# Four heads at a time in two cross attentions, a new order in the latents' attention, and half of X's norm first, in a Perceiver kernel of twelve blocks

## The chip, the cores and the metric

The kernel runs on one core of a Trainium2 chip, in one launch. The metric is device time in microseconds (us); less is better. A core has a matrix engine, TensorE (PE in profiles, with its weight loads under PEld), a vector engine (DVE), a scalar engine (ACT), GpSimd (POOL) and SyncE (SP), which here only issues DMAs. PE writes to PSUM; the other engines copy from there to SBUF, the working memory. Each engine has its own instruction stream and waits on semaphores for the others.

## The reference

Sixteen batch elements of 64 latent tokens with 256 channels (`x`) attend to 1024 context tokens of 192 channels, in four rounds of attention to the context, a mixing layer and a feed-forward layer:

```python
x = x + _L0_xattn_ref(_layernorm(x), ctx, ...)      # 16 heads of 16
x = x + _L0_attn_ref(_layernorm(x), ...)            # then _L0_ffn_ref
x = x + _L1_xattn_ref(_layernorm(x), ctx, ...)      # 8 heads of 64
x = x + _L1_attn_ref(_layernorm(x), ...)            # then _L1_ffn_ref
x = x + _L2_xattn_ref(_layernorm(x), ctx, ...)      # 8 heads of 64
x = x + _L2_attn_ref(_layernorm(x), ...)            # then _L2_ffn_ref
x = x + _L3_xattn_ref(ctx, _layernorm(x), mask, ...)  # 4 heads of 64
x = x + _L3_attn_ref(_layernorm(x), ...)            # then _L3_ffn_ref
```

The first three cross attentions are softmax attentions with the products

```python
q = (x @ Wq).reshape(B, Sq, h, d).transpose(0, 2, 1, 3)
k = (context @ Wk).reshape(B, -1, h, d).transpose(0, 2, 1, 3)
v = (context @ Wv).reshape(B, -1, h, d).transpose(0, 2, 1, 3)
attn = softmax(einsum('bhid,bhjd->bhij', q, k) * scale)
out = einsum('bhij,bhjd->bhid', attn, v)            # then @ Wo
```

The fourth normalises the context, takes keys and values from both context and latents (1024 + 64 keys), divides queries and keys of each head by their root mean square, and masks part of the context.

## The kernel before

All is float32. `X` holds the 1024 tokens as eight tiles of 128 x 256. The blocks run one after the other (`BLOCKS`); the change touches three of their functions, and `network`, which loads X.

**What orders the work.** A framework sorts the instructions into each engine's stream by a simulated time, and a piece of text that stands earlier goes first among what is ready. Where a block has called `set_order(True)`, every matrix instruction through `mm` (L188) and `tr` (L191, a transpose by the identity), and every DVE and ACT instruction through `dve` and `act` (all recorded at L72), keeps the order of the text on its engine. Instructions through `nc.vector`, `nc.gpsimd` and the DMA issues are outside that order. Tiles come from pools with a given number of buffers; a new tile waits until the last user of its buffer is done.

**First attention, `xattn_direct` (L281 on).** Weights wq, wk, wv, wo are loaded through POOL's queue; two value tiles of 128 x 4096 are zeroed on POOL (L313), since each head's 16 value channels stand in a block of 32. `norm_T` normalises all of X: `layernorm` takes statistics of tiles (L220, L221), roots on POOL (`rsqrt`, L205 and L206, for tiles 0 to 3, 4 to 6 and 7), normalises (L227), and transposes each half (L251) into `xnT`. Then `queries(0, c)` for the first eight batch elements, the four pieces of `project(0, piece)` (two of keys, two of values), and 64 steps over (element, four heads): scores (two PSUM tiles), negated maxima (`least`, nm), exponentials (`exps`, with their sums), division (`shares`), transposes, and the values of the step before. Steps 4 to 7 take the queries of the other eight elements.

**Cross attentions two and three, `xattn_folded` (L479 on).** The key weights are folded into the queries (`qw`), so scores are taken with the context itself: `cT` is its transpose, with 128 channels as full rows and the other 64 stored in two row halves for two halves of the keys; `cx` is the context as it is. There are 64 steps (b, r), r being a pair of heads. `scores` fills one PSUM tile of 128 x 1024: two products over 128 rows, then two over 64 rows, which run side by side in the two row halves of the array (64*128 in the profile). `transposes` turns the probabilities into `pT`, through two PSUM buffers (`ps_t`), the first half copied by ACT, the second by DVE. `values(b - 1, r)` multiplies two key tiles of the element before: full products into `o0`, and products of 64 columns into `o1`, of which two run side by side (128*64). A step is

```python
nxt = scores(*ahead)
transposes(pTs[b][:, :, r * P : (r + 1) * P], pr)
nxt = exps(*nxt)
values(b - 1, r)
pr = shares(*nxt)
```

`ps_s` has two buffers for scores; so have `cT`, `cx` and `pT`. Attention three also calls `ctx_sigma` for each element at its load, which takes the context's statistics with `nc.vector` (L277, L278: eight of each), outside the order. Attention two works on the taps of the next block's convolution in steps 6 to 23 (`conv_taps`, POOL, ACT, POOL, DVE in turn) and issues `tap_rows` DMAs later. Every eighth element new queries are folded (`fresh`).

**Latents' attention, `xattn3` (L1448 on).** One pass over 16 elements. In the pass of element b the four pieces of keys and values of b + 1 are projected (`project`, pkv; DVE evicts), squared on ACT, summed on DVE and rooted on POOL (`roots`, L1522 and L1523), scaled on DVE (`scale`), and transposed (`keys_T`); the latents' own keys take the same way (`latents`, `lat`). `last_T` turns the last keys of b + 1 and the last probabilities of b, `probs_T` the other probabilities, `values` multiplies. `mid` has seven PSUM buffers.

Of the kernel before, what the change touches and what calls it, by code (L numbers as in the profile page):

```python
# [78 lines left out]
class Net:  # L79
# [201 lines left out]
    def xattn_direct(self, L):  # L281
# [10 lines left out]
        H = 16  # L292
        wq = self.w(a[f"{L}_Wq"].rearrange("(k p) n -> p k n", p=P), [P, 2, D], "wq")
        wk = self.w(a[f"{L}_Wk"].rearrange("(k p) n -> p k n", p=P), [P, 2, D], "wk")
        wv = self.w(a[f"{L}_Wv"].rearrange("(k p) n -> p k n", p=P), [P, 2, D], "wv")
        wo = self.w(a[f"{L}_Wo"].rearrange("(k p) n -> p k n", p=P), [P, 4, D], "wo")
        with ExitStack() as es:
# [12 lines left out]
            vs = []  # L310
            for i in range(2):
                v = one.tile([P, NKC, H, 32], F32, name=f"v{i}")
                nc.gpsimd.memset(v, 0.0)  # L313
                vs.append(v)

            self.norm_T(ps_t, "t")
# [19 lines left out]
            for c in range(4):  # L336
                queries(0, c)
# [99 lines left out]

            self.set_order(True)
            for piece in range(4):
                project(0, piece)  # L440
            steps = [(b, c) for b in range(B) for c in range(4)]
            pss = scores(0, 0)
            prs = [exps(pss[e], least(pss[e])) for e in range(2)]
            for p in prs:
                shares(*p)
            last = None
            for i, (b, c) in enumerate(steps):
# [18 lines left out]
                transposes(pT[:, :, 1, :], prs[1][0], 1, act.copy)  # L466
                if 4 <= i < 8:
                    queries(1, i - 4)
# [10 lines left out]
    def xattn_folded(self, L):  # L479
# [14 lines left out]
        with ExitStack() as es:  # L494
# [52 lines left out]
            def scores(b, r):  # L547
                if r == 0:
                    load(b)
                c0, c1 = ctxs[b]  # L550
                qw = qws[b // G]
                ps = ps_s.tile([P, S], F32, tag="s", name="pss")
                ql = [qw[:, i, b % G, 2 * r : 2 * r + 2, :].rearrange("p h q -> p (h q)") for i in range(2)]
                for n in range(2):
                    cols = slice(n * 512, (n + 1) * 512)
                    self.mm(ps[:, cols], ql[0], c0[:, cols], True, False)
                for n in range(2):
                    cols, rows = slice(n * 512, (n + 1) * 512), slice(n * 64, (n + 1) * 64)
                    self.mm(ps[:, cols], ql[1][rows], c1[rows, :], False, True)
                nm = self.small.tile([P, 1], F32, tag="nm", name="nm", bufs=4)  # L560
                dve.tensor_reduce(nm, ps, AX.X, ALU.max, negate=True)
                return ps, nm

            def exps(ps, nm):
                pr = thr.tile([P, S], F32, tag="pr", name="pr")
                sm = self.small.tile([P, 1], F32, tag="sm", name="sm", bufs=4)
                act.activation(pr, ps, AF.Exp, bias=nm, accum_out=sm)
                return pr, sm
# [14 lines left out]
            def values(b, r):  # L583

                if r == 0:
                    outs[b] = [ps_o.tile([P, 512], F32, tag=n, name=n) for n in ("o0", "o1")]
                o0, o1 = outs[b]
                for j in (2 * r, 2 * r + 1):
                    self.mm(o0, cxs[b][:, j, 0:P], pTs[b][:, j, :], j == 0, j == NKC - 1)
                for j in (2 * r, 2 * r + 1):  # L590
                    rows = slice((j % 2) * 64, (j % 2 + 1) * 64)
                    self.mm(o1[rows, :], cxs[b][:, j, P:C], pTs[b][:, j, :], j < 2, j >= NKC - 2)
# [33 lines left out]
            steps = [(b, r) for b in range(B) for r in range(4)]  # L626
            pr = shares(*exps(*scores(0, 0)))
            for i, (b, r) in enumerate(steps):
# [6 lines left out]
                transposes(pTs[b][:, :, r * P : (r + 1) * P], pr)  # L635
                if fresh:
                    nxt = scores(*ahead)
                if ahead:
                    nxt = exps(*nxt)
                if b > 0:  # L640
                    values(b - 1, r)
                    if r == 3:
                        keep(b - 1)
                if ahead:
                    pr = shares(*nxt)
                if b == 1 and r == 0:
                    self.add_row(f"{L}_bo", one)
                if r == 0 and b % G2 == 1 and b > 1:
                    output(b // G2 - 1)
                if L == "L1_xattn":  # L650

                    if i == 6:
                        taps = self.conv_taps(one, dve, act)
                    if 6 <= i < 24:
                        next(taps)
                    if 28 <= i < 28 + TQ // 2:
                        self.tap_rows(2 * (i - 28))
                        self.tap_rows(2 * (i - 28) + 1)
            for r in range(4):
                values(B - 1, r)  # L660
            keep(B - 1)
# [786 lines left out]
    def xattn3(self):  # L1448
# [14 lines left out]
        with ExitStack() as es:  # L1463
# [5 lines left out]
            if not hasattr(self, "wx"):  # L1469
                self.context_weights()(mid)  # L1470
# [122 lines left out]
            def last_T(b, keys, prs):  # L1593

                pt = mid.tile([P, 512], F32, tag="m", name="ptl")
                if keys:
                    for c in range(2):
                        turn(pt, c, pair(b, NKC, c))
                if prs:
                    st["pT"] = one.tile([P, 2, KT, P], F32, tag="pT", name="pT")  # L1600
                    for c in range(2):
                        turn(pt, 2 + c, prs[c][:, S:])
                    act.copy(st["pT"][:, :, NKC, :], pt[:, 2 * P :].rearrange("p (c q) -> p c q", c=2))
                if keys:
                    act.copy(st["kT"][:, :, S:], pt[:, : 2 * P].rearrange("p (c k) -> p c k", c=2))
# [124 lines left out]
            last_T(0, True, None)  # L1730
# [3 lines left out]
            for b in range(B):  # L1734
# [21 lines left out]
                if more:  # L1756
                    p0, lat = roots(*p0), roots(*lat)
                    p1 = project(b + 1, 1)
                    scale(*p0)
                dve.reciprocal(sums, sums)  # L1760
                if more:
                    p1 = square(*p1)
                act.mul(prs[0], prs[0], sums[:, 0:1])
                if more:
                    p1 = roots(*p1)
# [4 lines left out]
                if more:  # L1770
                    p2 = project(b + 1, 2)
                    scale(*p1)
# [3 lines left out]
                    keys_T(b + 1, 0, act.copy)  # L1776
                act.mul(prs[1], prs[1], sums[:, 1:2])
                if 1 <= b <= 3:
                    q = roots(*q)
                if more:  # L1780
                    p2 = roots(*square(*p2))
                    late = project(b + 1, 3)
                last_T(b + 1, more, prs)
                probs_T(0, prs[0])
                if more:
                    late = square(*late)
                    keys_T(b + 1, 1, dve.tensor_copy)
                    late = roots(*late)
                    scale(*p2)
                if 1 <= b <= 3:  # L1790
                    scale(*q)
                probs_T(1, prs[1])
                values(b, 0)
                if more:
                    keys_T(b + 1, 2, dve.tensor_copy)
# [4 lines left out]
                values(b, 1)  # L1800
# [745 lines left out]
def network(ctx: ExitStack, tc: tile.TileContext, a, out, blocks=BLOCKS):  # L2546
    n = Net(ctx, tc, a)
    for t in range(NT):
        tc.nc.sync.dma_start(out=n.X[:, t, :], in_=a["x"][t * P : (t + 1) * P, :])
# [27 lines left out]
```

## Time and profile before

| | us |
|---|---|
| median of 3 runs | 3303.53 |
| lowest, highest | 3290.88, 3317.2 |
| the profiled execution | 3300.39 |
| its span | 3298.7 |
| PE busy in it | 3085.0 (94%) |
| DVE busy | 1857.1 (56%) |
| ACT busy | 1213.9 (37%) |
| POOL busy | 723.5 (22%) |

The profile is of one execution. A group's row gives an engine, an operation, the tile written and the tile read (out<-in), how often, and its duration. In a timeline the columns are the start and the duration in us, the engine, the line and operation, the tiles, and in brackets how long the engine had been idle and what released it; equal instructions in a row are merged (x8). A window's row is the busy time of PE, PEld, DVE, ACT and POOL with the number of instructions in brackets, then the granted TensorE clock (1 is full speed), the DMAs' share and GB/s. A matrix instruction's recorded duration overlaps the next one's, so starts are compared, not durations. The mean granted clock was 0.959.

Where the stages touched lie in the span: first attention from the start to about 514 us, cross attention two from 755 to 1263, three from 1693 to 2201, the latents' attention from 2596 to 3007.

### The profile page before, as it was taken

To read this page: it belongs to the slowest core of one execution; us is meant where nothing else is said; L and a number is where in the kernel's file an instruction comes from. 1 tells how busy PE (TensorE), PEld (TensorE's weight loads), DVE (VectorE), ACT (ScalarE), POOL (GpSimd) and SP (SyncE) were. 2 spreads that over 40 slices of the span, in tenths; PEclk is the share of its full clock that TensorE was granted. 3 is DMA by queue.
4 is the path that set the end of the run, shared out by engine and by line. 5 is a ranking of instruction groups with operands and counts; after the bars stand their busy time and mean duration, and the time that the engine had idled before them with its cause. 6 is when DMAs were issued, how large, how long until landed. Compare 5 with 4: busy or idle time off the path is not lost.

```text
span 3298.7 us, 48631 instructions
## 1 busy us (share of the span) xinstructions
PE 3085.0 (94%) x20064; PEld 1753.1 (53%) x20064; DVE 1857.1 (56%) x3497; ACT 1213.9 (37%) x2093; POOL 723.5 (22%) x786
## 2 busy tenths in 40 slices
PE   7999999999999999979969999998999899998787
PEld 4666665664344344468834434434665454455676
DVE  6888885424444445961135545557884677775521
ACT  3555554213322221003322232228861254544211
POOL 1000003311200001014410000023771354441131
PEclk9999999999999999969989999998998999999889
DMA  2100000012122113027821111101111111110233
GB/s 71 32 29 30 31 24 11 20 48 79 58 76 73 59 38 78 20 84 288 294 89 58 49 52 54 48 17 34 45 52 34 64 61 55 58 51 14 83 110 118
DMA packets 64511, 213.63 MB, mean 65 GB/s; under 512 B 16433, under 2 KB 27556, under 8 KB 57378
## 3 DMA queue, kind: packets, MB, share of 16 engines
q1 hardware_dynamic: 37296, 106.13, 9.6%
q0 software_dynamic: 21840, 99.39, 9.0%
q10 hardware_dynamic: 5154, 5.01, 0.5%
q8 instruction: 159, 2.61, 0.3%
q14 instruction: 62, 0.51, 0.1%
HBM read 201.62 MB, written 12.66 MB: 65 GB/s over the span
## 4 chain that ended last, share of the span: by engine, by line
PE 78%; DVE 8%; issue 5%; POOL 5%; ACT 3%; DMA 1%; POOLq 0%; DVEq 0%; SPq 0%; ACTq 0%
PE pss L188 14%; PE o L188 13%; PE pst L191 8%; PE pu L188 6%; PE psp L188 5%; PE pd L188 5%; PE py L188 4%; PE psc L188 3%; POOL rnk L1523 2%; PE po L188 2%; PE pb L191 2%; PE psq L188 1%; PE pkv L188 1%; DVE pr L72 1%; DVE kk L72 1%
## 5 line engine op out<-in xcount | busy, mean ns | idle before, releaser
L72 DVE TENSOR_REDUCE nm<-pss 128x1 f32<-128x1024 f32 x256 | 307.4, 1222 | 349.6 <-PE pss L188 349.6
L72 ACT COPY pT<-pst 128x512 f32<-128x512 f32 x256 | 149.8, 585 | 688.8 <-PE pst L191 688.5
L188 PE MATMUL pss<-cT,qw 128*128 128x512 f32 (+1 forms) x1024 | 387.8, 628 | 1.6 <-ACT qw L72 1.6
L188 PE MATMUL o<-pT,cx 128*128 128x512 f32 (+1 forms) x1024 | 370.5, 606 | 0.0
L191 PEld LDWEIGHTS pst<-ident,pr 128*128 128x128 f32 x2048 | 219.8, 141 | 159.1 <-issue 100.1
L72 ACT ACTIVATE pr<-pss,nm 128x1024 f32<-128x1024 f32 x256 | 285.1, 1114 | 34.4 <-DVE nm L72 21.0
L191 PE MATMUL pst<-ident,pr 128*128 128x128 f32 x2048 | 281.0, 280 | 5.7 <-DVE v L72 1.6
L188 PEld LDWEIGHTS pss<-cT,qw 128*128 128x128 f32 (+1 forms) x1024 | 125.8, 187 | 251.1 <-issue 239.4
L188 PEld LDWEIGHTS o<-pT,cx 128*128 128x128 f32 (+1 forms) x1024 | 112.6, 162 | 166.3 <-issue 145.0
L72 DVE TENSOR_SCALAR pr<-pr,sm 128x1024 f32<-128x1024 f32 x256 | 193.1, 754 | 9.0
L188 PE MATMUL pkv<-wx,cT 128*128 128x512 f32 (+1 forms) x512 | 190.2, 623 | 0.6 <-issue 0.6
L205 POOL TENSOR_SCALAR rs<-mv 128x8 f32<-128x8 f32 (+3 forms) x53 | 10.2, 193 | 802.3 <-DVE mv L221 400.3
L72 DVE COPY pT<-pst 128x512 f32<-128x512 f32 x256 | 174.5, 682 | 8.6 <-PE pst L191 4.5
L72 DVE TENSOR_TENSOR_SCAN h<-dA,pb 128x512 f32<-128x512 f32 x128 | 154.7, 1217 | 15.9 <-PE pb L191 9.0
L1347 POOL TENSOR_TENSOR h<-h,cb 128x1024 f32<-128x1024 f32 x64 | 151.4, 2367 | 53.3 <-DVE h L72 51.3
L188 PE MATMUL pd<-wd,hT 128*128 128x256 f32 x656 | 149.3, 382 | 3.0 <-DVE hT L2391 1.4
L2203 DVE TENSOR_SCALAR y<-pd,row 128x256 f32<-128x256 f32 x39 | 18.9, 484 | 223.7 <-PE pd L188 223.7
L188 PEld LDWEIGHTS pd<-wd,hT 128*128 128x128 f32 x656 | 123.1, 190 | 31.3 <-DVE hT L2391 6.2
L1523 POOL TENSOR_TENSOR rnk<-rnk,mhalf 128x8 f32<-128x8 f32 (+1 forms) x84 | 130.2, 1550 | 7.0
L188 PE MATMUL py<-h,ident 128*128 128x512 f32 x256 | 131.1, 598 | 0.0
L188 PEld LDWEIGHTS pu<-xT,up 128*128 128x128 f32 x736 | 110.8, 192 | 21.8 <-ACT hT L2197 14.6
L188 PE MATMUL pu<-xT,up 128*128 128x128 f32 x736 | 121.2, 290 | 1.1 <-DVE xT L2189 0.5
(511 smaller groups left out, 5195.6 us busy)
## 6 DMA issues: line engine op xcount, KB each, us to landing
cT<-in_ctxT SPq DMA_DIRECT2D x64, 768.0 KB, 4.4
cx<-in_ctxP SPq DMA_DIRECT2D x32, 768.0 KB, 4.3
offb<-d_off SPq DMA_DIRECT2D x16, 576.0 KB, 3.7
cb<-d_C SPq DMA_DIRECT2D x16, 512.0 KB, 3.6
wu<-in_L_ffn_w POOLq DMA_DIRECT2D x8, 1024.0 KB, 5.7
wd<-in_L_ffn_w POOLq DMA_DIRECT2D x8, 1024.0 KB, 6.3
wc<-in_L_attn_conv_wT POOLq DMA_DIRECT2D x4, 1024.0 KB, 10.2
T<-d_T SPq DMA_DIRECT2D x8, 512.0 KB, 18.5
```

The costliest lines, as they stand in the source:

```text
L72: ins = getattr(self.engine, op)(*args, **kwargs)
L188: self.in_order(self.nc.tensor.matmul(out, lhsT=lhsT, rhs=rhs, start=start, stop=stop))
L191: self.in_order(self.nc.tensor.transpose(out, in_, self.ident))
L205: nc.gpsimd.tensor_scalar(t[:p, :n], in_, scale, eps, ALU.mult, ALU.add)
L1347: nc.gpsimd.tensor_tensor(hs[i], hs[i], cbs[hf, g], ALU.mult)
L1523: nc.gpsimd.tensor_tensor(r, r, self.mhalf[:, : n * H], ALU.pow)
L2203: nc.vector.tensor_scalar(y[:, i, :], po[:, i * D : (i + 1) * D], weight[:, g + i : g + i + 1], None, ALU.mult)
```

## The change

- First attention: wk is loaded before wq; X's tiles 4 to 7 come through ACT's DMA queue instead of SP's; only the half of the value tiles that values don't fill is zeroed, the second tile's after the first root. The norm is split: `norm(0)` and `normed(0)` for tiles 0 to 3 at the front, `norm(1)` in step 1 and `normed(1)` in step 2. The first two pieces of `project` come before the first queries, the other two after the first scores.
- Cross attentions two and three: 32 steps (b, h) of four heads. `scores` fills both PSUM tiles: full products of both, then the 64-row products of both. `values` keeps the full products; the 64-column products of an element are in `others`, once for each element. `pr` gets four buffers. The taps are taken two to a step in steps 3 to 11.
- Latents' attention: reciprocals and products of the two probability tiles are taken one at a time, `scale`, `keys_T`, `probs_T` and `values` stand in another order, `last_T` is split into `latents_T` and `last_T`, and the copies of the second and third keys go from DVE to ACT. The test for `wx` falls away; the weights are prepared in an earlier block either way.

```diff
-        for t in range(NT): tc.nc.sync.dma_start(out=n.X[:, t, :], ...)
+        (tc.nc.sync, tc.nc.scalar)[t // 4].dma_start(out=n.X[:, t, :], ...)
@@ xattn_direct
-                nc.gpsimd.memset(v, 0.0)
-            self.norm_T(ps_t, "t")
-            for c in range(4):
-                queries(0, c)
-            for piece in range(4):
-                project(0, piece)
+            nc.gpsimd.memset(vs[0][:, :, :, 16:], 0.0)
...
+            norm(0)
+            ins = nc.gpsimd.memset(vs[1][:, :, :, 16:], 0.0)
+            tc.add_manual_dep(ins.ins, self.last_root.ins.name, order, reason="after the norm")
+            normed(0)
+            project(0, 0)
+            project(0, 1)
+            for c in range(4):
+                queries(0, c)
             pss = scores(0, 0)
             prs = [exps(pss[e], least(pss[e])) for e in range(2)]
+            project(0, 2)
+            project(0, 3)
...
+                if i == 1:
+                    norm(1)
+                if i == 2:
+                    normed(1)
@@ xattn_folded
+                for ps, q in zip(pss, ql):
+                    for n in range(2):
+                        self.mm(ps[:, cols], q[0], c0[:, cols], True, False)
+                for ps, q in zip(pss, ql):
+                    for n in range(2):
+                        self.mm(ps[:, cols], q[1][rows], c1[rows, :], False, True)
...
+            def others(b):
+                for j in range(NKC):
+                    rows = slice((j % 2) * 64, (j % 2 + 1) * 64)
+                    self.mm(outs[b][1][rows, :], cxs[b][:, j, P:C], pTs[b][:, j, :], j < 2, j >= NKC - 2)
...
+                    nxt = scores(*ahead)
+                transposes(pTs[b][:, :, at[0]], prs[0])
+                if ahead and not fresh:
+                    nxt = [exps(*x) for x in nxt]
+                if b > 0:
+                    values(b - 1, 2 * h)
+                transposes(pTs[b][:, :, at[1]], prs[1])
+                if fresh:
+                    nxt = [exps(*x) for x in scores(*ahead)]
+                if b > 0:
+                    values(b - 1, 2 * h + 1)
+                    if h == 1:
+                        others(b - 1)
+                        keep(b - 1)
+                if ahead:
+                    prs = [shares(*x) for x in nxt]
@@ xattn3, one pass, the new order
+                dve.reciprocal(sums[:, 0:1], sums[:, 0:1])
+                act.mul(prs[0], prs[0], sums[:, 0:1])
+                    p1 = project(b + 1, 1)
+                dve.reciprocal(sums[:, 1:2], sums[:, 1:2])
+                    p1 = square(*p1)
+                act.mul(prs[1], prs[1], sums[:, 1:2])
+                    scale(*p0)
+                    p1 = roots(*p1)
+                    p2 = square(*project(b + 1, 2))
+                    scale(*lat)
+                    p2 = roots(*p2)
+                    late = project(b + 1, 3)
+                probs_T(0, prs[0])
+                    keys_T(b + 1, 0, act.copy)
+                last_T(prs)
+                    late = square(*late)
+                probs_T(1, prs[1])
+                    scale(*p1)
+                    late = roots(*late)
+                    scale(*p2)
+                    latents_T(b + 1)
+                    keys_T(b + 1, 1, act.copy)
+                values(b, 0)
+                values(b, 1)
+                    keys_T(b + 1, 2, act.copy)
+                    scale(*late)
```

## The prediction

> **What bounds the kernel now.** I read the page's busy shares and its chain first, then the windows of each stage, then the timelines inside the touched stages.
>
> ```profile
> PE 78%; DVE 8%; issue 5%; POOL 5%; ACT 3%; DMA 1%; POOLq 0%; DVEq 0%; SPq 0%; ACTq 0%
> ```
>
> TensorE (PE) ends the chain for 78% of the span, so a stage gains only where its PE stream gets shorter or stops waiting. The windows of cross attention two, cross attention three and the latents' attention (length, then PE, PEld, DVE, ACT and POOL busy):
>
> ```profile
> 755.00:1262.60 507.60, 498.23 (x1853) 210.53 (x1854) 221.61 (x362) 148.18 (x258) 40.59 (x57) 0.99 0.21 65
> 1693.00:2200.60 507.60, 497.97 (x1852) 210.10 (x1852) 252.55 (x590) 143.17 (x240) 48.40 (x56) 0.99 0.14 48
> 2596.20:3006.50 410.30, 369.84 (x2752) 193.41 (x2752) 294.34 (x719) 199.23 (x343) 192.93 (x225) 0.98 0.15 53
> ```
>
> The first two are PE from end to end; the third leaves PE idle for 40 us. But "busy" hides something: the weight loads (PEld) of one step of attention two.
>
> ```profile
> 886.18 0.30 PEld L188 LDWEIGHTS pss<-cT,qw 128*128 128x128 f32 x2 [0.81 <-issue]
> 886.71 0.19 PEld L188 LDWEIGHTS pss<-cT,qw 128*128 128x128 f32 x1 [0.24 <-issue]
> ...
> 888.09 0.30 PEld L188 LDWEIGHTS pss<-cT,qw 64*128 64x128 f32 x4 [0.76 <-issue]
> 889.15 0.86 PEld L191 LDWEIGHTS pst<-ident,pr 128*128 128x128 f32 x8 [0.76 <-issue]
> 889.97 0.30 PEld L188 LDWEIGHTS o<-pT,cx 128*128 128x128 f32 x2
> 890.51 0.19 PEld L188 LDWEIGHTS o<-pT,cx 128*128 128x128 f32 x1 [0.24 <-issue]
> ...
> 891.89 0.20 PEld L188 LDWEIGHTS o<-pT,cx 128*64 128x64 f32 x4 [0.76 <-issue]
> 892.90 0.19 PEld L188 LDWEIGHTS pss<-cT,qw 128*128 128x128 f32 x1 [0.81 <-ACT tapp L72]
> ```
>
> Each f32 product is two passes, and full-array passes follow at 0.43 us. At a change of tiling the load is not hidden: four full passes from 886.18 to 888.09 take 1.91, not 1.72; the 64-row pairs 1.06, not 0.86; eight transposes and the first load 0.93, not 0.87; the next full passes (PE from 890.08) 1.81; the 64-column pairs 1.01, not 0.86. That is 0.69 us of 6.72 per step, 0.35 for each excursion into a 64-row or a 64-column tiling.
>
> **The change part by part.**
>
> *Attentions two and three.* Now each of 64 steps makes one row excursion (scores) and one column excursion (values). Then 32 double steps make one row excursion each, and `others` makes one column excursion per batch element: 48 instead of 128. 80 x 0.347 = 27.8 us per attention, all on PE.
>
> Is the new step fed? I lay it out from its start S with the durations above. Score sums end at 4.75 and 5.6; DVE nm 4.8 to 7.2 (two take 2.36); PE transposes 5.55 to 6.48, values to 8.19, second transposes to 9.07, values to 10.8. ACT: pT copy at 6.15, exponentials 6.75 to 9.2, pT copy 9.25. DVE: pT copy 7.2 to 7.85, then 9.25 to 9.9, the two shares to 11.7. The second transposes need the buffer that DVE's copy frees at 7.85; they come at 8.19/8.63: slack 0.8. Both score tiles are free at 9.2, needed at 10.8. The shares are due at 16.3. Hidden, then. Attention two's taps, two per step: their chain POOL 0.62, ACT 0.41, POOL 1.18, DVE 0.42, twice, ends near 14.8 with the next nm ready at 15.3 (20.1 against 19.3 after a longer step, which the 0.8 of slack covers): nothing. Here the skill has a rule against the change: "TensorEngine Tiling (Array Packing)", section PSUM Bottleneck, warns that once tiling speeds up PE the copies out of PSUM can become the bound, which would make this part 0. The row says DVE is busy 221.61 of 507.60; I keep 27.8.
>
> *Costs of doing two at a time.* The first scores and their exponentials now occupy both score buffers, so PE waits 1.8 us for the first to free; in the first batch element, which has no values between its transposes, the second transposes wait 1.25 twice. Against 0.6 now: -3.7 per attention. Attention two: +24.
>
> *Attention three has a guest.* `ctx_sigma` runs on DVE outside the ordered queue:
>
> ```profile
> 1881.89 1.23 DVE L72 TENSOR_REDUCE nm<-pss 128x1 f32<-128x1024 f32 x1 [2.44 <-PE pss L188]
> 1883.25 0.62 DVE L277 BATCH_NORM_STATS2 st<-cx 128x6 f32<-128x192 f32 x2
> ...
> 1885.82 0.66 DVE L72 COPY pT<-pst 128x512 f32<-128x512 f32 x1
> ```
>
> The context's load is issued when the old values end (1878.92, with S at 1878.80) and its 16 small operations (2.65 us) start on landing, 4.4 later, ahead of the pT copy. Today the next transposes come 6.7 us apart and hide this. In the new step they land at S+4.45, before the first nm: nm 7.1 to 9.5, copy to 10.2, and the second transposes, due at 8.63, start at 10.3. That is 1.65 us of PE wait for each of the 14 batch elements whose context waits for a buffer: -23. If the operations fall behind one or both nm it is 2.0 (-28); if behind the pT copy, nothing. I take -23: attention three +1.
>
> A wait can also cost clock. Windows of 3.41 us, the granted clock being the third number from the end:
>
> ```profile
> 2623.66:2627.07 3.41, 1.65 (x11) 1.05 (x8) 2.23 (x8) 0.58 (x1) 1.04 (x1) 1.00 0.00 0
> 2627.07:2630.48 3.41, 3.41 (x23) 1.05 (x23) 3.19 (x10) 0.10 (x1) 1.20 (x2) 1.00 0.00 0
> ...
> 3009.36:3012.78 3.42, 1.30 (x3) 0.68 (x4) 2.41 (x5) 0.00 (x0) 2.26 (x6) 1.00 0.26 53
> 3012.78:3016.19 3.41, 3.41 (x9) 2.26 (x8) 1.03 (x3) 1.46 (x4) 0.00 (x0) 0.50 0.62 255
> ```
>
> 1.76 us idle in a window left the clock whole, 2.11 halved the next one (1.7 us lost). The skill ("TensorE: Matmul & The Clock Gate", HAM oscillation) names only gaps over about 3.4 us; by it the wait costs itself alone, by these rows a wait of 2.1 adds up to 14 x 1.7 = 24. At 1.65 both give 0, so 0 stands and 24 goes into the range.
>
> *Latents' attention.* The waits of one batch element:
>
> ```profile
> 2882.01 0.63 PE L191 MATMUL ptk<-ident,kk 128*128 128x128 f32 x4 [0.48 <-DVE sums L72]
> 2886.36 0.41 PE L191 MATMUL ptl<-ident,kk 128*128 128x128 f32 x2 [0.95 <-DVE kk L72]
> 2890.64 0.63 PE L191 MATMUL ptk<-ident,kk 128*128 128x128 f32 x4 [0.27 <-DVE kk L72]
> ```
>
> 1.69 us in each from the fourth to the fifteenth; scale waits on POOL's roots (1.66 each), and PE's transposes wait on scale. In the new order, from the start of scores: fourth projection ends 14.6, first probabilities' transposes then (their product is done by 11.2), first keys 15.6 (scale 11.9), last and second probabilities to 17.2 (12.9), latents and second keys to 17.9 (scale 17.3), values to 20.4 (ACT copies 18.8), third keys (scale 19.0) to 20.9. The split of `last_T` takes one more PSUM tile, 24 in turn over seven buffers, each free before its turn by at least 0.3. No wait is left; what is latest is scale of the fourth piece, 21.2 against 21.9. DVE loses two copies (0.69), ACT gains them (0.56) and has room. Two values in a row save one tiling change, about 0.15. 12 x 1.84 = 22, plus some 1.4 for each of the second and third, 1 for the first, 1.2 at the end, where the first transposes no longer wait for the second product (1.25): 27.2. Discount for a wait that I missed: 25.5, bounds 12 and 28.
>
> *First attention's front.* PE starts at 15.37 because:
>
> ```profile
> 5.41 6.98 POOL L313 MEMSET v<- 128x4096 f32 x2
> ...
> 13.80 1.89 POOL L206 TENSOR_TENSOR rstd<-rs,mhalf 128x4 f32<-128x4 f32 x2
> ```
>
> Half a memset is 1.75 (3.5 if stride costs as much): POOL free at 7.2 to 8.9. Statistics of four tiles end at 7.6. With the root (0.2 + 1.06, plus 0.77 if the wdt load is again issued in between) and four normalisations of 0.34, first projections start between 11.5 and 13.5; the context, landed 8.7 us after its issue at 5.73, is issued some 2 us earlier, behind four X loads, the other four on ACT's queue behind pcol, pbc and downb (issued by 2.33). wk goes before wq, each an issue of 0.8 on POOL; four X issues of 0.43 on ACT end long before its first copy at 17.6. I take 12.5. From there: two key pieces 5.9 (+1.2 for the half clock that now ends at 19.3), four queries 6.9, scores 1.0, two value pieces 6.0, then steps of 7.7, 7.0 and 10.8, the last ones lengthened by the second half's norm on DVE (2.25 + 1.4) and its transposes. The fifth scores start at 58.8, against 65.1 now: +6, bounds 2 and 9. The second memset, after the root, is covered by 30 us of steps before its tile is used.
>
> Moved to the side at no cost: SP issues attention loads when their buffer frees, the cT of two elements ahead at 1868.44 before the cx at 1878.92; the new lead is 2.5 double steps against a landing of 4.3.
>
> **Sum.** 6 + 24 + 1 + 25.5 = 56.5 us from the profiled 3300.4 (span 3298.7): 3244. The median of the runs shown is 3.1 above it: 3246.
>
> **The rivals.**
> - *Attention three gains like two* (its statistics fall behind the pT copy). For: nothing orders them. Against: they stood before that copy in every element. 3246 - 23 = 3223.
> - *Waits grow*: attention three's reaches 2.1 and halves windows (+24), or half of the latents' waits survive (+13). 3270.
> - *Drains stay*: two score tiles side by side still pay each change of tiling. 3246 + 56 = 3302. Against: the 64-row pairs follow at full rate within a run now.
> - *Slower: context late.* If SP issued in the program's order, a cT would stand behind a cx that waits for `others`, with one step of 10.8 us left. It decides from a landing over 10.8 (two together took 8.7); 3 us late in 28 loads is 84: 3330. Against: the issue order above.
>
> **How the numbers follow.** The likeliest 50% (3232 to 3262), attention three gaining 22%, waits grow 17%, drains stay 6%, slower 5%. A difference under 1% (33 us) can't be told from none by this measurement. Faster by over 1%: 50 + 22 + 12 = 84%; within 1%: 11%; slower: 5%. 3214 to 3278 leaves out about one in five.
>
> **What would show it.** Attention two's stage near 483 us; its second transposes without waits. Attention three near 506, with PE waiting some 1.6 us on pT once per element; without that wait, the first rival. Latents' period down from 22.5 to about 20.7 (plus output and latents). Fifth scores of attention one near 59. Wrong if loads (cT) end PE's waits, or 64-row loads still start 0.2 late per head pair.

## The result and the profile after

| | before | after |
|---|---|---|
| median of 4 runs each, us | 3297.2 | 3253.5 |
| lowest, highest | 3288.09, 3317.2 | 3237.14, 3266.45 |
| profiled execution, us (span) | 3300.39 (3298.7) | 3253.72 (3252.0) |
| mean granted clock in it | 0.959 | 0.955 |

The ratio is 0.9861, with a 95% interval of 0.9823 to 0.9899; five later runs of the same kernel gave 3248.07 us, 0.983 (0.9799 to 0.9861) of before. The kernel is faster by 1.4 to 1.7%: 44 to 55 us, where 57 were forecast.

First the share line of the chain of waits, after:

```profile
PE 79%; DVE 9%; issue 4%; DMA 3%; POOL 2%; ACT 2%; ACTq 0%; POOLq 0%; DVEq 0%; SPq 0%
```

PE still ends the chain, so the stages can be compared by PE's starts. The same three windows as before the change, each cut at the same work as then (length; PE, PEld, DVE, ACT and POOL busy; clock; DMAs). Attention three's start is set by its query products (PE at 1703.62 before, at 1690.04 after), since the norm ahead of them lies 0.5 us differently in a half-clock stretch:

```profile
755.60:1239.60 484.00, 472.39 (x1853) 223.68 (x1854) 218.42 (x362) 139.56 (x258) 35.49 (x57) 0.99 0.21 68
1679.40:2184.30 504.90, 475.68 (x1851) 223.22 (x1852) 247.71 (x587) 136.05 (x240) 43.61 (x56) 0.99 0.14 48
2576.40:2965.10 388.70, 369.42 (x2752) 193.35 (x2752) 273.66 (x705) 211.67 (x373) 195.59 (x225) 0.98 0.16 56
```

Attention two went from 507.60 to 484.00, attention three only from 507.60 to 504.90, the latents' attention from 410.30 to 388.70. Attentions two and three do the same products, but PE is busy for 475.68 us of 504.90 in three, so idle for 29, and idle for only 12 in two. The timeline shows where, in one first double step (VectorE's and PE's lines; the other small statistics are left out):

```profile
1838.83 0.62 DVE L277 BATCH_NORM_STATS2 st<-cx 128x6 f32<-128x192 f32 x2 [5.31 <-DMA cx<-in_ctxP]
...
1840.14 1.09 PE L191 MATMUL pst<-ident,pr 128*128 128x128 f32 x8
...
1841.40 1.19 DVE L72 TENSOR_REDUCE nm<-pss 128x1 f32<-128x1024 f32 x1
...
1842.60 1.20 DVE L72 TENSOR_REDUCE nm<-pss 128x1 f32<-128x1024 f32 x1
...
1843.70 0.69 DVE L72 COPY pT<-pst 128x512 f32<-128x512 f32 x1
...
1844.45 0.66 PE L191 MATMUL pst<-ident,pr 128*128 128x128 f32 x4 [1.05 <-DVE pT L72]
```

Read it from the bottom. Ahead of the second four transposes PE stands idle for 1.05 us, until DVE has copied the first transposes' second half out (`pT`). That copy's input was complete at about 1841.2, but DVE came to it at 1843.70: from 1838.83, when the context landed, it took statistics, and then the two maxima that had become ready meanwhile and stand ahead of the copy in the order. This is the wait that the prediction laid out, in its order.

The front of the first attention (POOL's lines, then PE's first two groups):

```profile
5.41 1.82 POOL L311 MEMSET v<- 128x2048 f32 x1
7.33 0.19 POOL L205 TENSOR_SCALAR rs<-mv 128x4 f32<-128x4 f32 x1
7.59 0.77 POOL L169 DMA_DIRECT2D wdt<-in_L_attn_in_proj_wT  x1
8.38 1.06 POOL L206 TENSOR_TENSOR rs<-rs,mhalf 128x4 f32<-128x4 f32 x1
...
11.41 2.29 PE L191 MATMUL psT<-ident,xn 128*128 128x128 f32 x8 [11.41 <-DVE xn L72]
...
13.63 3.91 PE L188 MATMUL psp<-cT,wk 128*64 128x512 f32 x12
```

Half a memset cost 1.82 (half of the earlier 3.49 is 1.75), so the strided destination cost almost nothing. The wdt load did fall between the two parts of the root. PE starts at 11.41, not 15.37, and the fifth scores at 59.64, not 65.09: 5.45 earlier.

For the latents' attention, the list of PE's waits over ten of the pass's steady elements (total, times, longest, in us), before:

```profile
PE ptl L191 <- DVE kk L72: 9.4, 10, 0.9
PE ptk L191 <- DVE sums L72: 4.8, 10, 0.5
PE ptk L191 <- DVE kk L72: 4.2, 11, 1.5
```

and after:

```profile
PE ptk L191 <- PE pss L188: 0.9, 5, 0.2
PE ptk L191 <- DVE kk L72: 0.5, 1, 0.5
```

**The account.** Offsets of equal PE instructions between the two traces give the measured column, by stage:

| | forecast | measured |
|---|---|---|
| first attention's front | -6 | -5.45 |
| attention two | -24 | -23.6 |
| attention three | -1 | -2.7 |
| latents' attention | -25.5 | -21.6 |
| sum of the touched stages | -56.5 | -53.4 |
| everything else | 0 | +6.7 |
| span | -56.5 | -46.7 |

The last but one line is granted clock, not work: outside the touched stages the after trace has 10 us more lost to half clock. Two consecutive windows of the first attention, before:

```profile
299.18:302.59 3.41, 2.94 (x76) 2.01 (x75) 3.41 (x6) 1.27 (x3) 0.00 (x0) 1.00 0.00 0
302.59:306.01 3.42, 2.14 (x16) 1.15 (x16) 3.27 (x7) 2.12 (x4) 0.00 (x0) 1.00 0.00 0
```

and the same work after:

```profile
296.34:299.76 3.42, 1.67 (x36) 1.11 (x24) 3.35 (x7) 2.33 (x5) 0.00 (x0) 1.00 0.00 0
299.76:303.17 3.41, 3.41 (x15) 1.91 (x16) 2.15 (x4) 0.92 (x2) 0.00 (x0) 0.50 0.00 0
```

The clock is granted anew every 3.41 us: the half-clock stretches inside both traces last that long or a whole multiple of it, up to 47.8 us. PE has the same two waits in both kernels (0.95 and 0.80 us); before, the border of two windows fell between them, and after, 5.45 us earlier against another grid, both fell into one, and the next window ran at half clock. That the grid decides, and not the kernel, the second profile of the changed kernel shows (`e9_after_again`), where a border lies between the same two waits again and no window is halved:

```profile
294.03:297.44 3.41, 3.13 (x77) 2.20 (x75) 3.41 (x7) 1.07 (x2) 0.00 (x0) 1.00 0.00 0
297.44:300.85 3.41, 1.94 (x16) 1.15 (x16) 3.34 (x8) 2.32 (x6) 0.00 (x0) 1.00 0.00 0
300.85:304.27 3.42, 3.42 (x25) 2.56 (x20) 3.05 (x5) 2.25 (x4) 0.00 (x0) 1.00 0.03 7
```

Two such places (at 300 and 559 us), a half-clock stretch that lasts 10.2 us in place of 3.4 (at 604) and a much longer one (below) cost 15 us ahead of attentions two and three. Later stages get 9 of that back, most of it by fewer half-clock windows.

This also explains the scatter. Over runs of one kernel the time goes with the mean granted clock, and their product is steady: span times clock was 3157.5 to 3167.4 us over 45 runs of before (mean 3163.2), a range of 10 us, while their spans had one of over 40. I use this product as a second measure. Each clock is given to three digits, so that one run's product is uncertain by 1.6 us and a mean over five by less than 1; an idle microsecond inside a half-clock window counts as half. After, it is 3110.0 over nine runs (3101.6 to 3113.3): 53.2 us less, about the sum of the touched stages.

### The profile page after: what moved, and what is told of

Its sections match the earlier page's. It is cut to its first block, busy times and chain, and to the rows that moved or that the text cites. A ratio compares the mean times of both kernels' runs of the same rounds, so it can differ in the third digit from the quotient of the medians.

```text
span 3252.0 us, 48672 instructions
## 1 busy us (share of the span) xinstructions
PE 3043.1 (94%) x20064; PEld 1783.0 (55%) x20064; DVE 1830.0 (56%) x3483; ACT 1210.3 (37%) x2123; POOL 712.3 (22%) x784
## 4 chain that ended last, share of the span: by engine, by line
PE 79%; DVE 9%; issue 4%; DMA 3%; POOL 2%; ACT 2%; ACTq 0%; POOLq 0%; DVEq 0%; SPq 0%
PE o L188 12%; PE pss L188 12%; PE pst L191 7%; PE pu L188 6%; PE psp L188 5%; PE pd L188 5%; PE pkv L188 5%; PE py L188 4%; PE psc L188 3%; PE po L188 2%; DMA cx<-in_ctxP 2%; DVE nm L72 2%; PE pb L191 2%; PE psq L188 2%; PE psi L188 1%
## 5 line engine op out<-in xcount | busy, mean ns | idle before, releaser
L188 PE MATMUL pss<-cT,qw 128*128 128x512 f32 (+1 forms) x1024 | 356.2, 607 | 5.0 <-ACT pr L72 3.4
L188 PE MATMUL o<-pT,cx 128*64 128x512 f32 (+1 forms) x1024 | 354.9, 596 | 0.0
L188 PEld LDWEIGHTS pss<-cT,qw 128*128 128x128 f32 (+1 forms) x1024 | 138.2, 188 | 211.5 <-issue 201.9
L188 PEld LDWEIGHTS o<-pT,cx 128*64 128x64 f32 (+1 forms) x1024 | 121.7, 163 | 146.3 <-issue 146.3
L72 DVE TENSOR_TENSOR_SCAN h<-dA,pb 128x512 f32<-128x512 f32 x128 | 154.7, 1217 | 15.6 <-PE pb L191 9.3
L2254 DVE TENSOR_SCALAR y<-pd,row 128x256 f32<-128x256 f32 x39 | 18.9, 484 | 222.7 <-PE pd L188 222.7
L188 PEld LDWEIGHTS pkv<-wx,cT 128*128 128x128 f32 (+1 forms) x512 | 63.6, 187 | 116.8 <-issue 90.7
L188 PEld LDWEIGHTS pu<-xT,up 128*128 128x128 f32 x736 | 110.8, 192 | 21.6 <-ACT hT L2248 14.5
```

The costliest lines, as they stand in the source:

```text
L72: ins = getattr(self.engine, op)(*args, **kwargs)
L188: self.in_order(self.nc.tensor.matmul(out, lhsT=lhsT, rhs=rhs, start=start, stop=stop))
L2254: nc.vector.tensor_scalar(y[:, i, :], po[:, i * D : (i + 1) * D], weight[:, g + i : g + i + 1], None, ALU.mult)
```

## The experiments

Stages are compared by PE's starts against those of before, each in one profile, times by medians, and "product" is span times mean clock.

**One part of the change at a time** (before, with one of the three functions as after; the front with X's load).

> The kernel before with only the new step of cross attentions two and three. If the gain is that of the saved tiling changes (80 of 0.35 us in each attention, less the slower start) and attention three gives it back to 14 waits for pT, attention two gets 23 to 24 us shorter (507.6 to about 484) and attention three 1 to 4 us (to about 504 to 506), as in the changed kernel (23.6 and 2.7), and the whole 25 to 27 us. Rival, drains stay: both stages within 4 us of before, the whole unchanged. Rival, attention three's small gain came from the changed stages before it (another phase of its loads) and not from its own step: it gains about 20 here.

> The kernel before with only the latents' attention in its new order. If the order alone is the cause: period of two elements down from 47.6 to 44.5 us, the stage 21 to 22 us shorter, as in the changed kernel. Rival: part of that stage's gain comes of the other changes (its weights or context arriving earlier or later), then the stage gains under 15 or over 27 here. By the prediction's sum it would be 27.

> The kernel before with only the front of the first attention (the order of X's load with it). If the front's 5.5 us are gained there and given back where short waits of PE now fall into one clock window in place of two, the scores of the steps near 80 us stand 5.5 us earlier than before, and the first attention's end less than that: -5.5 + 0 to 6 us, the whole within 10 us of before on either side. Rival: the new order leaves a steady cost in the steps of the first attention (its queues or buffers), then the offset to before shrinks evenly over the 64 steps and not in jumps at half-clock windows.

| | median of n runs, us | product (before 3163.1) | touched stage |
|---|---|---|---|
| attentions two and three alone | 3279.65 of 13 | 3136.5 (-26.6) | -23.6 and -3.2 |
| latents' attention alone | 3274.82 of 7 | 3141.0 (-22.1) | -18.9 |
| front alone | 3297.6 of 12 | 3159.7 (-3.4) | -4.5 |
| before, same chip | 3295.13 of 27 | 3163.1 | |

Attentions two and three give the same alone as in the whole; what was done ahead of them has no part in it. By its median this kernel gained 15.5 us, where 25 to 27 had been expected; by the product it gained 26.6. The latents' stage was to be 21 to 22 shorter and came out at 18.9, because its second element took 28.69 us in place of the 25.71 of the changed kernel, over two half-clock windows that the other trace doesn't have there; the steady elements alternate between 20.83 and 23.64 us in both kernels (22.50 and 25.09 before). So the order alone is the cause, and the 3 us go with those windows. The front's offset stays at -4.50 us from 84 us of the span to 484, so that the even loss of the rival isn't there; but in the profiled run a later loop fell into half clock early and lost up to 15.6 us against before, and over 12 runs the median is no better than before. The three products add up to -52.1, against -53.2 for the whole.

**Who makes attention three wait.** The statistics go through the ordered queue, behind the shares of the element's first double step:

```diff
-            nc.vector.bn_stats(st[:, j, :], cx[:, j, :])
-            nc.vector.bn_aggr(mv[:, j, :], st[:, j, :])
+            dve.bn_stats(st[:, j, :], cx[:, j, :])
+            dve.bn_aggr(mv[:, j, :], st[:, j, :])
@@ scores
-                if L == "L2_xattn":
-                    self.ctx_sigma(b, cxs[b])
@@ the double step, behind shares
+                if h == 0 and L == "L2_xattn":
+                    self.ctx_sigma(b, cxs[b], dve)
```

> The changed kernel with the context's statistics in attention three put in the DVE's ordered stream behind the shares of the element's first double step, so that they can't stand ahead of the pT copy. If these 16 operations are what PE waits for, the waits ahead of the second transposes vanish and attention three falls from about 505 us to 483 to 486 like attention two, the whole by 19 to 22 us against the changed kernel. Rival: PE waits there for nm or for the exponentials whatever the statistics do: the stage stays within 4 us of the changed kernel's. Third: they delay the next nm instead, then waits turn up at the scores or at the first transposes of the following double step, and half or less is gained.

The stage was 14.8 us shorter than before, 12.1 less than in the changed kernel, and the median 3237.38 (4 runs). In the list of PE's waits in it (total, times, longest, in us), the waits on pT, in the changed kernel

```profile
PE pst L191 <- DVE pT L72: 18.1, 16, 2.3
```

have all but gone, and there is a new first line:

```profile
PE psy L188 <- DVE oT L72: 4.9, 3, 1.6
...
PE pst L191 <- DVE pT L72: 2.0, 2, 1.8
```

One of the three, in the timeline (DVE's statistics of 3.8 us, then its copy for the output's second product):

```profile
1841.50 0.35 DVE L72 BATCH_NORM_STATS2 st<-cx 128x6 f32<-128x192 f32 x1
...
1845.27 0.66 DVE L72 COPY oT<-pso 128x512 f32<-128x512 f32 x1
...
1846.08 3.69 PE L188 MATMUL psy<-wo,oT 128*128 128x256 f32 x16 [1.62 <-DVE oT L72]
```

Every fourth element has its output projected in that very double step, and its copy now stood behind the statistics. That is a fourth outcome, which none of the expectations had named: the waits for pT were the statistics' doing, and the statistics, once moved, held up the next thing on VectorE. Two edits follow: the second double step, which has no output, and the eight statistics of one kind ahead of the eight of the other, since each of the second kind reads what the first has just written.

```diff
         for j in range(NKC):
             dve.bn_stats(st[:, j, :], cx[:, j, :])
+        for j in range(NKC):
             dve.bn_aggr(mv[:, j, :], st[:, j, :])
@@ the double step, behind shares
-                if h == 0 and L == "L2_xattn":
+                if h == 1 and L == "L2_xattn":
```

> The changed kernel with attention three's context statistics in the DVE's ordered stream behind the shares of each element's second double step (the eight of one kind, then the eight of the other). Behind the first double step they had taken away all 14 waits for pT but put three waits of 1.6 us on the output's projections, which stand in that same step. If that was all, the second double step has room from 11.7 to 15.5 us after its start: no wait for pT, none for oT, attention three 20 to 22 us shorter than before (23 if it gains like two, 2.7 in the changed kernel), the whole about 18 us under the changed kernel. Rival: the statistics now end behind the next element's first nm is due (they took 4.1 us there, there are 3.8): waits of up to 0.5 us at the scores or the second transposes, 14 of them, and a stage only 14 to 16 us shorter.

> The changed kernel once more, for more runs of it: 3237 to 3266 us, a span times mean clock of 3104 to 3112 us (3107.9 over its four runs), with the stages of the touched attentions as in its profile (23.6, 2.7 and 21.6 us shorter than before) and the difference between runs in half-clock stretches outside them. Rival: the stages themselves differ between runs of one kernel by several us.

With the statistics behind the second double step (e8), attention three, from the same work to the same work:

```profile
1675.90:2159.60 483.70, 472.20 (x1851) 223.57 (x1852) 249.29 (x587) 133.54 (x240) 44.64 (x56) 0.99 0.14 50
```

and the statistics in their new place:

```profile
1856.79 2.17 DVE L72 BATCH_NORM_STATS2 st<-cx 128x6 f32<-128x192 f32 x8
1858.88 0.63 DVE L72 BATCH_NORM_AGGREGATE mv<-st 128x2 f32<-128x6 f32 x8
...
1862.75 2.36 DVE L72 TENSOR_REDUCE nm<-pss 128x1 f32<-128x1024 f32 x2 [3.25 <-PE pss L188]
```

483.70 us, 23.9 less than before: attention three gains what attention two does. The statistics take 2.72 us in this order, and DVE is idle for 3.25 before the next maxima. The median of five runs is 3228.29, a ratio of 0.9779 (0.974 to 0.9818) to before; the changed kernel beside it had 3248.07. Products: 3090.0 and 3111.6. From 504.9 to 483.7 makes 21.2 us, or 1.51 for each of 14 waits; the idle time recorded for them is less (18.1 in the changed kernel's list of waits, 0.6 left in this one's), since records overlap their neighbours: by PE's starts, the changed kernel falls behind this one by 20.0 us in fourteen jumps, each at second transposes. The changed kernel's own second profile (e9) has the touched stages 23.7, 3.2 and 21.6 us shorter than before, like the first.

**The suspected cost once more, in attention two.** The statistics are taken there too (the same values, twice; a single profiled run):

```diff
-                if L == "L2_xattn":
-                    self.ctx_sigma(b, cxs[b])
+                self.ctx_sigma(b, cxs[b])
```

> The changed kernel with the context's statistics also taken in attention two, at each element's load as in attention three (the same values, taken twice). If they and nothing else set attention three apart from two, attention two now has 14 waits of 1 to 1.5 us ahead of its second transposes too and loses 17 to 21 us: 3 to 7 us shorter than before in place of 23.6. Rival: the waits belong to attention three's own loads and queues; attention two changes by under 4 us.

```profile
751.60:1266.20 514.60, 478.48 (x1853) 224.59 (x1854) 258.53 (x618) 142.40 (x258) 65.03 (x89) 0.98 0.20 64
```

Attention two is 30.6 us longer than in the changed kernel, and so 7.0 longer than before, where 3 to 7 shorter was expected. Thirteen waits of 0.9 to 1.5 us have appeared before its second transposes, like attention three's; at 1.51 they make 20, as expected. The rest comes of one wait that was not expected:

```profile
973.84 0.52 SPq L572 DMA_DIRECT2D cx<-in_ctxP  x1
...
978.10 0.62 DVE L277 BATCH_NORM_STATS2 st<-cx 128x6 f32<-128x192 f32 x2 [12.34 <-DMA cx<-in_ctxP]
...
983.71 1.11 PE L191 MATMUL pst<-ident,pr 128*128 128x128 f32 x4 [8.09 <-DVE pT L72]
```

SP had been issuing `tap_rows` DMAs (38 of them in 25.0 us) and came to this context late. DVE holds the statistics' place in its stream, stands idle for 12.34 us until the context lands, and the copy that PE needs is behind it. A half-clock stretch follows (978 to 989). So work that waits for a DMA blocked everything behind it on its engine, ready or not; in attention three no such issues are in SP's way.

**What an excursion costs.** Two kernels, of each a single profiled run: each score tile's own 64-row products behind its own full products (one more row excursion for each double step, 32 in all), and the 64-column products in fours behind each pair of heads (64 column excursions in place of 16):

```diff
@@ scores apart
                         self.mm(ps[:, cols], q[0], c0[:, cols], True, False)
-                for ps, q in zip(pss, ql):
                     for n in range(2):
@@ columns spread
-            def others(b):
-                for j in range(NKC):
+            def others(b, r):
+                for j in (2 * r, 2 * r + 1):
...
                 if b > 0:
                     values(b - 1, 2 * h)
+                    others(b - 1, 2 * h)
...
                     values(b - 1, 2 * h + 1)
+                    others(b - 1, 2 * h + 1)
```

> The changed kernel with each score tile's products over 128 rows followed by its own over 64 rows, so that each double step has one more excursion into the row tiling. If an excursion costs 0.35 us, attention two gets 32 x 0.35 = 11 us longer than in the changed kernel (12.5 shorter than before in place of 23.6). In attention three the first score tile is then ready 2.1 us sooner, its nm would stand ahead of the statistics and the pT copy in time for the second transposes: +11 there and up to 17 of waits gone, so from 5 us shorter to 11 us longer. Rival, the gain came of something else than the tiling changes (fewer steps, larger slack): attention two stays within 3 us.

> The changed kernel with the products of 64 columns again in fours behind the values of each pair of heads, so 64 excursions into the column tiling in each attention in place of 16. If such an excursion costs the 0.35 us of the sum, attention two gets 48 x 0.347 = 16.7 us longer than in the changed kernel (some 7 us shorter than before in place of 23.6), and attention three by as much less what its pT waits shrink by, since the second transposes come later against the statistics in each first double step by 0.35 plus 0.5 us of the products that now stand ahead of them: 16.7 less 0 to 7. Rival, only the row excursions were worth something: under 3 us in attention two.

Attention two with the scores apart:

```profile
750.70:1245.20 494.50, 485.44 (x1853) 218.47 (x1854) 220.06 (x361) 139.90 (x258) 35.57 (x57) 0.99 0.21 66
```

and with the columns spread:

```profile
749.60:1247.50 497.90, 486.34 (x1853) 215.91 (x1854) 217.50 (x362) 142.65 (x258) 36.52 (x57) 0.99 0.21 66
```

The first is 10.5 us longer than the changed kernel's stage. It also starts better: PE's wait of 1.71 us for a score buffer at the stage's start is gone, and half of four small ones with it (0.24 to 0.28 each), so 12.7 us are the 32 excursions: 0.40 each. The second is 13.9 us longer, 0.29 for each of 48. The prediction had read 0.347 for both from one timeline: right in the mean (0.33), 0.05 off on either side. Kept apart, its five differences say as much: 0.19 and 0.20 at the 64-row products, 0.09 and 0.15 at the 64-column ones, 0.06 at the transposes between them.

In attention three both missed. With the scores apart the stage was 12.5 us shorter than before, 9.8 less than in the changed kernel, where 5 less to 11 more was expected: the waits for pT are gone there from the second element on, and they were worth some 20 us (9.8 and 10.5), not 17 at most. With the columns spread it was 6.0 shorter than before, 3.3 *less* than in the changed kernel, where some 10 to 17 more was expected: the 64-column products and their excursion (0.86 and 0.29) now stand ahead of the second transposes, and behind the first element no wait for pT over 0.2 was left. Fewer tiling changes had uncovered the wait.

**Does the front last?** The best kernel so far with the old front, beside the same kernel with the new one on the same chip. The edit takes the front's part of the change back.

> The kernel with the statistics behind the second double step, but with the front of the first attention (and the order of X's load) as before the change. If the front's 5 us of earlier steps last to the end, span times mean clock is 3 to 6 us above that of the same kernel with the new front (3090), and the median of times too, on a mean over runs. Rival: nothing of it lasts, since waits elsewhere or half-clock stretches take it back; both means within 2 us.

> The kernel with the statistics behind the second double step once more, beside the one with the old front on the same chip: 3217 to 3242 us, span times mean clock 3088 to 3093, attention three 23 to 24.5 us shorter than before, no wait for pT in it. Rival: its 20 us under the changed kernel came of the chip or of half-clock stretches, and half or less of it returns.

Old front: 3244.06 us (3237.28 to 3258.83), clock 0.953 in the mean of five runs, product 3090.3. New front: 3229.86 (3226.59 to 3237.44), clock 0.957, product 3090.2; its ratio to before is 0.9804 (0.9788 to 0.982), and its attention three again 23.9 us shorter. By the product the front is worth nothing, by the times 14 us, and in the experiment with the front alone it was 3.4 and nothing; 3 to 6 in both had been expected if it lasts. PE surely starts its steps earlier (3.4 to 5.5 us, 4.7 on average, in the nine profiles with the new front; 0.7 later than before on average in the four with the old one, so 5.4 between them), but half-clock stretches later on can outweigh that: one, in a loop shown in the last section, lasted 54.6 us in the profile with the old front and 13.7 in the one with the new. What the front is worth on its own isn't settled by these runs.

## Why the prediction was right

The forecast was 3246 us, in a range of 3214 to 3278; measured were 3253.5 and, in the second set, 3248.07. The likeliest case came true in the mechanism of each of its parts, and none of the rivals did. How close the number came is in part luck: the median of the changed kernel itself moved by 5.4 us between the two sets, whose mean clocks were 0.956 and 0.959. (The last step of the sum, 3244 and 3.1, makes 3247, not 3246.)

- *Attention two, -24*: -23.6. Both terms were a little large and cancelled. The saved excursions are 32 x 0.40 + 48 x 0.29 = 26.7 by the experiments, not 27.8. The slower start, put at 3.7, has 1.71 for the score buffer (1.8 forecast) and four waits of 0.26, less the 0.6 saved, 2.2 in all: where the forecast had 1.25 twice, PE waited 0.24 and 0.28, twice each. 26.7 less 2.2 is 24.5; 0.9 of it isn't accounted for. The taps cost nothing, as worked out: no wait for them stands in this stage. Neither did copies out of PSUM become the bound, the rule that was weighed and set aside: DVE is busy 218.42 of 484.00.
- *Attention three, -1*: -2.7. The mechanism was right in its order (statistics on landing, maxima, copy, transposes), and moving, doubling and outrunning the statistics each showed it. The size: 14 x 1.65 = 23 forecast, 14 x 1.51 = 21.2 measured against the kernel without these waits. The rival in which it gains like two was wrong for this kernel, and right for the one in which the statistics are put behind the shares. No wait of this kind halved a window.
- *Latents' attention, -25.5*: -21.6, the term that was mis-sized; its 3.9 us are more than the 3.1 between the sums. 1.84 for each steady element was 1.69 of idle and 0.15 of a tiling change; measured are 1.67 and 1.45 in turn (22.50 to 20.83, 25.09 to 23.64), 1.56 on average. The idle time did go, and the two values in a row do save it: 2.25 us for both together after, against 1.24 and 1.19. What takes some of it back wasn't in the sum: the second keys' transposes start 0.44 us after the latents' begin, where 0.22 had been the spacing (their scale ends just then), and the fourth projection, which now follows the third directly, takes 2.97 us where one that stands alone takes 2.87. "No wait is left" was nearly true: 0.2 us in every other element. At the end, 1.2 us were forecast for transposes that no longer wait for the second product; PE's wait for it had been 0.67 us (at 2999.02 before), and the way from the last scores to the stage's end got only 0.1 shorter (16.23 to 16.14), with 0.9 us more of that work in a half-clock stretch. The discount for a missed wait was right in kind and too small.
- *Front, -6*: -5.45 at the fifth scores (59.64, with 58.8 forecast, where the terms add up to 59.0), and 4.7 on average over the profiles with this front.
- *Nothing elsewhere*: +6.7 in the profiled run, all of it in half-clock windows of stages that weren't touched. The sum had no term for it. Over the runs it is no steady cost: 53.2 us in the product, 44 and 55 in the two comparisons of medians.
- *The moved loads at no cost*: no wait of PE on cT or cx in either attention. The slower rival, a context that comes late behind other issues of SP, didn't happen in the changed kernel; its mechanism was seen once, at 8.09 us, when statistics in attention two made DVE depend on such a load.

## What to carry to other kernels

When a step is made longer to save changes of tiling, lay out every engine's work inside the new step, guests included that no order holds: here VectorE's statistics, hidden under a step of 6.7 us, took back seven eighths of one attention's gain, and placing them by hand behind the last ordered piece of work of a step without an output returned 20 us. A placement is only as good as the next thing on that engine, so look at the double step with the most work, not at the typical one. And where waits of about a microsecond are spread over a kernel, compare stages, or span times clock, since the same waits against another clock grid moved the total by more than single parts of the change.

## What the hardware showed that was not expected

The prediction held a window of 1.76 us idle to be harmless and one of 2.11 not. At 296 us above, a window with 1.75 us idle was followed by a half one. Elsewhere the next window stayed whole after 2.01 us (at 2459 us with the scores apart) and was halved after 0.79 (at 42 us with the latents' attention alone). So the idle time of a window alone doesn't decide. The Trainium skill's rule that the prediction weighed ("TensorE: Matmul & The Clock Gate", HAM oscillation) names single gaps of over about 3.4 us; here two of 0.95 and 0.80 us went ahead of a half-clock window.

The largest loss has no wait at all. A mixing stage between the two attentions runs a loop of small products (64 x 64 weights, 8 columns) in turn with full ones. Its timeline after, around the drop:

```profile
1378.42 1.10 PE L188 MATMUL psT<-xt,T 64*64 64x8 f32 x32
1379.45 1.13 PE L188 MATMUL psi<-xnT,w_in 128*128 128x512 f32 x2
...
1383.35 1.88 PE L188 MATMUL psT<-xt,T 64*64 64x8 f32 x32
...
1385.16 2.07 PE L188 MATMUL psi<-xnT,w_in 128*128 128x512 f32 x2
```

PE shows no idle time in it, yet from 1381.8 the clock is half until shortly behind the loop's end (1412.5, 30.7 us). A pair takes 3.81 us in place of 2.09. Before, the same loop dropped only in its last two pairs (1415.3 to 1425.6); with the old front on the best kernel it lay in half clock from 1377 to 1431. Once down it never came back within the loop, and where it drops differs from run to run. What goes ahead of the drop can be read from the windows:

```profile
1374.95:1378.37 3.42, 3.42 (x50) 1.91 (x48) 3.42 (x5) 0.09 (x1) 0.00 (x0) 1.00 0.03 5
1378.37:1381.78 3.41, 3.41 (x68) 2.56 (x68) 3.41 (x5) 1.06 (x2) 0.00 (x0) 1.00 0.00 0
1381.78:1385.19 3.41, 3.41 (x35) 1.89 (x34) 3.41 (x6) 0.69 (x1) 0.00 (x0) 0.50 0.00 0
```

By PE's starts, the second of them holds 64 of the small products, 2.06 us of its 3.41; the first holds 40, 1.36 us. In all thirteen profiles the loop's last window at full clock holds 62 to 64 of them (1.99 to 2.06 us), and of 68 other full-clock windows with these products only two hold as many. So the drop goes with how much of one window they take, and the grid decides where two whole groups fall into one. That they are the reason is likely by this, but not shown: no run changed them.
